# Order of work inside the slots of a selective scan: decays, first columns and the chain that makes dt

## The chip, the cores and the metric

The kernel runs on one NeuronCore of one Trainium2 chip. Its engines are named as the profile names them: PE (TensorE, matmuls; PEld is its weight load), DVE (VectorE), ACT (ScalarE), POOL (GpSimd) and SP (SyncE, which here issues nearly all DMAs). Each engine works off its own queue in order: an instruction that waits holds up everything behind it on that engine. The metric is the device time of one launch in microseconds (us), the median of several runs.

## What is computed

A network of four layers (each an attention-like block and a feed-forward block with a layer norm after each) on an input of 2 x 1024 x 1024 in float32. Only layer 2's first block, a selective state-space scan over 1024 time steps, matters here. Cut to its core:

```python
def _selective_scan(x, dt, A, Bm, Cm):
    def step(h, inp):
        x_t, dt_t, B_t, C_t = inp
        dA = jnp.exp(dt_t[..., None] * A)
        dBx = dt_t[..., None] * B_t[:, None, :] * x_t[..., None]
        h = dA * h + dBx
        y = jnp.einsum('bdn,bn->bd', h, C_t)
        return (h, y)
    h0 = jnp.zeros((x.shape[0], x.shape[1], A.shape[1]), dtype=x.dtype)
    _, ys = lax.scan(step, h0, (xT, dtT, BT, CT))
    return jnp.transpose(ys, (1, 2, 0))
...
dt = jax.nn.softplus(dt + dt_bias[None, :, None])
ys = _selective_scan(xc, dt, A, Bm, Cm)
y = (ys + D_param[None, :, None] * xc) * jax.nn.silu(z)
return jnp.einsum('bdl,hd->blh', y, out_proj_w)
```

There are 2048 channels d with 16 states n each, so 32,768 recurrences of 1024 steps for each batch element.

## The kernel before, in words

The two batch elements are done one after the other, all layers of one before the next (`net_kernel`). `l2_attn` does the scan of one batch element. Time is cut into two halves of 512 steps, u=0 and u=1; channels into 16 chunks c of 128. A chunk of one half is worked off in eight **slots**; a slot k is 128 x 2 recurrences: a tile `h` of 128 partitions (8 channels x 16 states) by 2 x 512 steps, whose two parts are called m=0 and m=1. So a batch element has 2 x 16 x 8 = 256 slots, and a run-in of 23 slots before them. All tiles of a slot, and where they come from:

- `rows(k)` (L1269) loads `h` from DRAM: dt times x of 16 channels (`dxd`), each row repeated for the 16 states (DMA at L1273, 512 KB). Nine such buffers exist.
- `times_b(k)` (L1278) multiplies it by B on POOL (L1279).
- `decay(k, m)` (L1283): a matmul (L1286) spreads dt's channels over the partitions into a PSUM bank, in two parts `hl` that carry dt's high and low bits; ACT then takes exp with scale A in place (L1288). For u=1 ACT also adds the state that u=0 left (`hst`), times the first decay, to the first column of `h` (L1291): the "first-column operation". A scan always starts from zero, so this carries the state over.
- `scan(k, m)` (L1293) is one DVE instruction (L1296): h = dA * h + h along the 512 steps.
- `keep(k)` (L1300) saves the last column for u=1 (L1304, u=0 only); `times_c(k)` multiplies by C on DVE (L1307); `states(k)` (L1311) sums over the 16 states by matmuls with a selection matrix (L1318), and a first matmul (L1316) adds D times x; `y_out` (L1328) multiplies by the gate and stores.

The chain that makes dt for a chunk is `l2_dt` (L1208), called 16 slots ahead of the chunk's first slot. Its matmul (L1211) gives the argument of the softplus; the rest is put off to later slots with `at(slot, function)`: softplus(p) is relu(p) + ln(1 + exp(-|p|)) with a correction of the rounding in 1 + exp(-|p|). `act1` and `act2` are three ACT operations each (L1221 to L1228), `pool1` two on POOL (L1231, L1232), `sum1` adds relu (L1235), `times_x` multiplies by x (L1238) and stores `dxd` in four DMAs (L1240); `parts` casts dt into the high part of `hl` (L1247), `rest` takes the low part (L1252), and `send` copies it into place by two DMAs (L1258). The tile `one` of this chain has one buffer, which `y_out` uses too.

The order of the work is written out by hand: inside `manual_schedule`, every engine's queue has the order in which the program issues. A slot issues, in this order: `rows(k+6)`, `times_b(k+2)`, `keep(k-1)`, a projection matmul (`pe()`); then scan(k,0), decay(k+1,0), the functions that were put off to this slot (`late.pop(k)`), another projection matmul; then scan(k,1), decay(k+1,1), and `states` and `times_c(k-1)`. The projection matmuls belong to other work that fills PE during the scans: the gates z (copied out by ACT at L1414), the next half's x (a convolution on DVE, L1124, and a silu), the output projection (L1441); `silu_z` (L1384) does silus between two loads of activation tables (L1388, L193). They put their later steps off with `at` as well. All PSUM tiles of the kernel, the decays' among them, come from one pool of eight banks (L43, `ps()` at L70).

Of the kernel before, what the change touches and what calls it, by code (L numbers as in the profile page):

```python
# [11 lines left out]
AF = mybir.ActivationFunctionType  # L12
# [15 lines left out]
class Net:  # L28
# [1032 lines left out]
    def l2_attn(self, b, ready, last):  # L1061
        nc, i = self.nc, self.i
        NCH, N, NR = 16, 16, 64
        NF = NR + 2 * N
        SL = 8 * NCH
        with (
# [24 lines left out]
            hst = lp.tile([P, NCH * N], F, name=self.nm("hst"))  # L1091

            def tmp(tag, bufs=2, n=HALF):
                return tp.tile([P, n], F, tag=tag, bufs=bufs, name=self.nm(tag))

            def dram(tag, shape, dtype=F):
                return [[self.dp.tile(shape, dtype, name=self.nm(tag)) for _ in range(NCH)] for _ in range(2)]

            xcd, yd = [dram(t, [P, HALF]) for t in ("xcd", "yd")]
# [3 lines left out]
            px, norms, hl, hs, dA, py, xs = {}, {}, {}, {}, {}, {}, {}  # L1103
# [6 lines left out]
            def at(k, f, *args):  # L1110
                late.setdefault(k, []).append((f, args))
# [96 lines left out]
            def l2_dt(u, c, k):  # L1208

                p = self.ps()  # L1210
                nc.tensor.matmul(  # L1211
                    p, wd[c // 8][: NF + 1, (c % 8) * P : (c % 8 + 1) * P], norms[u][0], start=True, stop=True
                )
                xs[u, c] = xc = tmp("xi")
                at(k + 3, nc.sync.dma_start, xc, xcd[u][c][:])
                e, one, lg = tmp("e", 1), tmp("one", 1), tmp("lg", 1)
                dt, dtx = lg, e
                rl = tmp("rl", 1)

                def act1():  # L1220
                    nc.scalar.activation(rl, p, AF.Relu)  # L1221
                    nc.scalar.activation(e, p, AF.Abs)
                    nc.scalar.activation(e, e, AF.Exp, scale=-1.0)

                def act2():
                    nc.scalar.activation(one, e, AF.Identity, bias=self.one)
                    nc.scalar.activation(lg, one, AF.Ln)
                    nc.scalar.activation(one, one, AF.Identity, bias=neg)  # L1228

                def pool1():  # L1230
                    nc.gpsimd.tensor_tensor(e, e, one, ALU.subtract)  # L1231
                    nc.gpsimd.tensor_tensor(lg, lg, e, ALU.add)  # L1232

                def sum1():
                    nc.gpsimd.tensor_tensor(dt, lg, rl, ALU.add)  # L1235

                def times_x():
                    nc.gpsimd.tensor_tensor(dtx, dt, xc, ALU.mult)  # L1238
                    for j in range(4):
                        nc.sync.dma_start(dxd[u][c][:, j, :], dtx[32 * j : 32 * j + 32, :])  # L1240

                low = [None]

                def parts():

                    hl[u, c] = tp.tile([P, 2, HALF], R, tag="hl", bufs=2, name=self.nm("hl"))
                    nc.scalar.copy(hl[u, c], dt.unsqueeze(1).to_broadcast([P, 2, HALF]))  # L1247

                def rest():

                    lo = low[0] = tp.tile([P, HALF], R, tag="lo", bufs=1, name=self.nm("lo"))
                    nc.gpsimd.tensor_tensor(lo, dt, hl[u, c][:, 0, :].bitcast(F), ALU.subtract)  # L1252

                def send():

                    lo = low[0]
                    for j in range(2):
                        nc.sync.dma_start(  # L1258
                            hl[u, c][64 - 64 * j : P - 64 * j, j, :].bitcast(F), lo[64 * j : 64 * j + 64, :].bitcast(F)
                        )  # L1260

                for n, f in ((1, act1), (2, act2), (3, pool1), (4, sum1), (5, times_x), (7, parts), (7, rest), (8, send)):
                    at(k + n, f)


            def of(k):
                return k // SL, k % SL // 8, k % 8 // 2, k % 2
# [15 lines left out]
            def decay(k, m):  # L1283
                u, c, q, jj = of(k)
                dA[k, m] = self.ps()
                nc.tensor.matmul(dA[k, m], rep[:, 4 * m + q, :], hl[u, c][:, jj, :], start=True, stop=True)  # L1286
                g = 16 * c + 4 * q + 2 * jj + m
                nc.scalar.activation(dA[k, m], dA[k, m], AF.Exp, scale=A[:, g : g + 1])  # L1288
                if u:
                    h0 = hs[k][:, m, 0:1]  # L1290
                    nc.scalar.activation(h0, dA[k, m][:, 0:1], AF.Identity, scale=hst[:, g : g + 1], bias=h0)  # L1291

            def scan(k, m):  # L1293
                u, c, q, jj = of(k)
# [33 lines left out]
            def y_out(k):  # L1328
                u, c = k // SL, k % SL // 8
                sz = zt.pop((u, c))  # L1330
                yo = tmp("one", 1)
                nc.scalar.copy(yo, py.pop((u, c)))
                nc.gpsimd.tensor_tensor(sz, sz, yo, ALU.mult)
                nc.sync.dma_start(yd[u][c][:], sz)
# [127 lines left out]
            with self.tc.manual_schedule():  # L1462

                todo, ahead = [], []

                def take(units, lead):
                    for n, (load, calls) in enumerate(units):
                        ahead.append((len(todo) - lead, load))
                        todo.extend(calls)

                z0, z1, x1 = gates(0), gates(1), ins(1)
                take(z0[:2] + x1[:6], 20)
                for n in range(2, 12, 2):
                    take(z0[n : n + 2] + x1[n + 4 : n + 6], 20)
                take(xproj(1), 4)
                take(z0[12:] + z1[:6], 20)
                taken = 0
                at(-BEFORE, lambda: at(4 - BEFORE, l2_spread, 0, l2_norm(0)))
                for k in range(-BEFORE, 2 * SL + 6):
                    if -16 <= k < 2 * SL - 16 and k % 8 == 0:  # L1480
                        l2_dt((k + 16) // SL, (k + 16) % SL // 8, k)
                    if k == SL + 12:
                        o = outs(0)
                        for n, (a, z) in enumerate(((6, 10), (10, 12), (12, 16), (16, 16))):
                            take(o[8 * n : 8 * n + 8], 8)
                            take(z1[a:z], 20)
                    if k == -1 or k == SL:
                        l2_cr(max(k, 0) // SL)
                    n = 3 if k < -1 else 2
                    batch = []  # L1490
                    for _ in range(n):
                        while ahead and ahead[0][0] <= taken:
                            ahead.pop(0)[1]()
                        if taken < len(todo):
                            batch.append(todo[taken])
                            taken += 1

                    def pe(last=False):
                        while batch and (last or len(batch) > n - 1):
                            f, *args = batch.pop(0)  # L1500
                            if f:
                                f(*args, k)

                    live = 0 <= k < 2 * SL
                    if 0 <= k + 6 < 2 * SL:
                        rows(k + 6)
                    if 0 <= k + 2 < 2 * SL:
                        times_b(k + 2)
                    if 0 <= k - 1 < 2 * SL:
                        keep(k - 1)  # L1510
                    pe()
                    for m in range(2):
                        if live:
                            scan(k, m)
                        if 0 <= k + 1 < 2 * SL:
                            decay(k + 1, m)
                        if m:
                            break
                        for f, args in late.pop(k, []):
                            f(*args)  # L1520
                        pe(True)
                    if k % 2 == 1 and 0 <= k - 2 < 2 * SL:
                        states(k - 2)
                    if 0 <= k - 1 < 2 * SL:
                        times_c(k - 1)
                    if live and k % 8 == 4:
                        at(k + 8, y_out, k)
                    if live and k % 8 == 0:
                        skip(k // SL, k % SL // 8)
                while late:  # L1530
                    for f, args in late.pop(min(late)):
                        f(*args)
# [460 lines left out]
```

## Time and profile before

| | us |
|---|---|
| median of 3 runs (lowest, highest) | 5127.48 (5123.48, 5133.85) |
| the profiled execution | 5130.32 |
| its span, first to last instruction | 5128.4 |
| scan stage of the first batch element | about 1050 to 2005 |
| scan stage of the second | about 3600 to 4547 |
| busy in the whole span: PE, DVE, ACT, POOL | 4706.3, 3128.0, 2109.7, 2097.7 |

The overview of the page cuts the span into 40 slices of 128 us; each digit is a slice's busy share in tenths:

```profile
PE   8989989998897888999999999899888988899999
DVE  5453256389999997225365422652899999963153
ACT  2431232377677774001024311424776777720010
POOL 2013121078798885100020220200887998831010
DMA  2144212388889998201111432113888899971100
```

In the rest of the kernel PE is busy nearly all the time; in the two scan stages all five rows are high at once. In the rows of groups, the first numbers after the bar are busy us and mean ns of one instruction; after the second bar stands the idle time of the engine just before them, with the instruction that ended most of it. In rows of the timeline the columns are start and duration in us, engine, line, operation, tiles and shapes, count, and in brackets idle time before it and its releaser. A busy PE is modelled and not a PE at its peak.

### The profile page before, as it was taken

To read this page: it belongs to the slowest core of one execution; us is meant where nothing else is said; L and a number is where in the kernel's file an instruction comes from. 1 tells how busy PE (TensorE), PEld (TensorE's weight loads), DVE (VectorE), ACT (ScalarE), POOL (GpSimd) and SP (SyncE) were. 2 spreads that over 40 slices of the span, in tenths; PEclk is the share of its full clock that TensorE was granted. 3 is DMA by queue.
4 is the path that set the end of the run, shared out by engine and by line. 5 is a ranking of instruction groups with operands and counts; after the bars stand their busy time and mean duration, and the time that the engine had idled before them with its cause. 6 is when DMAs were issued, how large, how long until landed. Compare 5 with 4: busy or idle time off the path is not lost. (4 is left out here: it accounts for less than half of the span.)

```text
span 5128.4 us, 50257 instructions
## 1 busy us (share of the span) xinstructions
PE 4706.3 (92%) x16584; PEld 2237.2 (44%) x16584; DVE 3128.0 (61%) x4322; ACT 2109.7 (41%) x4485; POOL 2097.7 (41%) x1259
## 2 busy tenths in 40 slices
PE   8989989998897888999999999899888988899999
PEld 3347645433332333455433576554333333344544
DVE  5453256389999997225365422652899999963153
ACT  2431232377677774001024311424776777720010
POOL 2013121078798885100020220200887998831010
PEclk9999999999999999999999999999999999999999
DMA  2144212388889998201111432113888899971100
GB/s 88 36 159 143 97 48 81 131 216 217 220 225 242 236 244 226 90 33 46 49 67 38 173 119 89 54 51 103 220 219 224 214 247 245 249 210 65 55 20 33
DMA packets 254871, 708.06 MB, mean 138 GB/s; under 512 B 37008, under 2 KB 54544, under 8 KB 254612
## 3 DMA queue, kind: packets, MB, share of 16 engines
q1 hardware_dynamic: 248340, 683.88, 46.7%
q0 software_dynamic: 6272, 20.98, 1.2%
q8 instruction: 133, 2.18, 0.2%
q14 instruction: 126, 1.03, 0.1%
HBM read 599.60 MB, written 86.25 MB: 134 GB/s over the span
## 5 line engine op out<-in xcount | busy, mean ns | idle before, releaser
L1296 DVE TENSOR_TENSOR_SCAN h<-ps,h 128x512 f32<-128x512 f32 x1024 | 1204.1, 1207 | 88.9 <-ACT h L1291 47.2
L1279 POOL TENSOR_TENSOR h<-h,br 128x1024 f32<-128x1024 f32 x512 | 1201.0, 2367 | 43.3 <-DMA h<-dxd 20.7
L1286 PE MATMUL ps<-hl,rep 128*128 128x512 f32 x1024 | 717.9, 708 | 119.9 <-DVE h L1296 94.7
L1288 ACT ACTIVATE ps<-ps,l_Alog 128x512 f32<-128x512 f32 x1024 | 667.9, 657 | 216.9 <-PE ps L1286 213.6
L1307 DVE TENSOR_TENSOR h<-h,ps 128x1024 f32<-128x1024 f32 x512 | 610.8, 1193 | 0.0
L1403 PE MATMUL ps<-xT,w 128*128 128x512 f32 x1024 | 541.1, 615 | 10.2 <-DVE h L1296 7.9
L1608 POOL TENSOR_TENSOR x<-x,row 128x1024 f32<-128x1024 f32 x48 | 112.3, 2349 | 796.0 <-PE ps L130 796.0
L1286 PEld LDWEIGHTS ps<-hl,rep 128*128 128x128 f32 x1024 | 198.6, 195 | 523.6 <-DVE h L1296 340.1
L152 DVE TENSOR_TENSOR x<-x,ps 128x512 f32<-128x512 f32 x192 | 128.4, 681 | 434.4 <-PE ps L1785 145.6
L1318 PE MATMUL ps<-h,sel 128*32 128x512 f32 x2048 | 365.1, 638 | 18.8 <-DVE h L1307 18.2
L104 PE MATMUL ps<-xT,w 128*128 128x512 f32 x768 | 336.1, 592 | 0.0
L177 ACT ACTIVATE rs<-mv 128x1 f32<-128x1 f32 (+2 forms) x88 | 17.9, 203 | 705.7 <-DVE mv L171 705.4
L1441 PE MATMUL ps<-w,w 128*128 128x512 f32 x512 | 279.9, 630 | 20.8 <-DMA w<-yd 12.1
L1403 PEld LDWEIGHTS ps<-xT,w 128*128 128x128 f32 x1024 | 190.6, 195 | 204.2 <-issue 136.7
L104 PE MATMUL ps<-w,xT 128*128 128x512 f32 (+1 forms) x768 | 278.3, 522 | 0.0
L1124 DVE SCALAR_TENSOR_TENSOR ps<-xp,l_convw,ps 128x512 f32<-128x512 f32 x192 | 144.4, 752 | 213.4 <-ACT ps L1119 208.9
L767 POOL TENSOR_TENSOR s<-s,l1r 128x512 f32<-128x512 f32 x64 | 66.5, 1040 | 487.7 <-DVE l1r L766 481.8
L1349 PE MATMUL ps<-xT,w 128*128 128x512 f32 x512 | 251.9, 602 | 0.7
L1291 ACT ACTIVATE h<-ps,h,hst 128x1 f32<-128x1 f32 x512 | 180.0, 352 | 118.5 <-POOL h L1279 93.9
L1782 PE MATMUL ps<-w,xT 128*128 128x512 f32 x512 | 227.4, 597 | 0.0
L1622 PE MATMUL ps<-w,w 128*128 128x512 f32 x512 | 222.6, 594 | 4.2 <-DMA w<-yd 4.2
L104 PEld LDWEIGHTS ps<-xT,w 128*128 128x128 f32 x768 | 144.8, 189 | 183.4 <-issue 177.6
(289 smaller groups left out, 7319.9 us busy)
## 6 DMA issues: line engine op xcount, KB each, us to landing
h<-dxd SPq DMA_DIRECT2D x512, 512.0 KB, 7.2
w<-l_in SPq DMA_DIRECT2D x128, 512.0 KB, 6.7
w<-l_out SPq DMA_DIRECT2D x96, 512.0 KB, 6.2
w<-l_conv SPq DMA_DIRECT2D x54, 512.0 KB, 3.9
w<-cvd SPq DMA_DIRECT2D x36, 512.0 KB, 3.3
w<-l_fw SPq DMA_DIRECT2D x32, 512.0 KB, 4.4
xcd<-xo SPq DMA_DIRECT2D x64, 256.0 KB, 2.2
xi<-xcd SPq DMA_DIRECT2D x64, 256.0 KB, 5.4
```

What stands on the lines that cost most here:

```text
L104: self.nc.tensor.matmul(out, lhsT, rhs, start=j == 0, stop=j == n - 1)
L1279: nc.gpsimd.tensor_tensor(hs[k], hs[k], norms[of(k)[0]][1].unsqueeze(1).to_broadcast([P, 2, HALF]), ALU.mult)
L1286: nc.tensor.matmul(dA[k, m], rep[:, 4 * m + q, :], hl[u, c][:, jj, :], start=True, stop=True)
L1288: nc.scalar.activation(dA[k, m], dA[k, m], AF.Exp, scale=A[:, g : g + 1])
L1296: nc.vector.tensor_tensor_scan(hs[k][:, m, :], dA.pop((k, m)), hs[k][:, m, :], 0.0, ALU.mult, ALU.add)
L1307: nc.vector.tensor_tensor(hs[k], hs[k], norms[of(k)[0]][3].unsqueeze(1).to_broadcast([P, 2, HALF]), ALU.mult)
L1318: nc.tensor.matmul(py[u, c][32 * j : 32 * j + 32, :], self.sel[:, q, :], hs[k - 1 + j // 2][:, j % 2, :], start=False, stop=q == 3,)
L1349: nc.tensor.matmul(p, w["w"][:, k * P : (k + 1) * P], self.xcols(k, u0, HALF), start=k == 0, stop=k == KD - 1)
L1403: nc.tensor.matmul(p, w["w"][:, k * P : (k + 1) * P], self.xcols(k, u * HALF, HALF), start=k == 0, stop=k == KD - 1)
L1441: nc.tensor.matmul(p, y[:, cc, t * P : (t + 1) * P], wt[:, cc * HALF : (cc + 1) * HALF], start=c2 == 0 and cc == 0, stop=last,)
L1622: nc.tensor.matmul(acc[tt], y[:, cc * HALF + tt * P : cc * HALF + (tt + 1) * P], w[:, cc * HALF : (cc + 1) * HALF], start=c == 0, stop=c = ...
L1782: nc.tensor.matmul(p, self.xcols(k, tt * P, P), wt[k][:, ns], start=k == 0, stop=False)
```

## The change

Three things in `l2_attn` and a buffer that they need. No operation is added or dropped.

- Decays: scan(k,0) is followed by decay(k+1,1) and scan(k,1) by decay(k+2,0), instead of decay(k+1,0) and decay(k+1,1).
- First columns: both of slot k+1 are issued together by a new `begin(k+1)`, after scan(k,0) and decay(k+1,1) and ahead of the functions put off to the slot.
- The chain of dt: its ACT operations take five slots (1 to 5, two operations in the first) instead of two, POOL's two log operations slots 5 and 6 instead of both in 3; the sum comes in slot 7 instead of 4, `times_x` in 8 instead of 5, `parts` in 8 instead of 7, `rest` in 9 instead of 7, `send` in 10 instead of 8. x is loaded in slot 4 instead of 3. The product with x is written to `one` instead of `e`, and `y_out` has a buffer of its own, `yo`.

```diff
@@ l2_dt(u, c, k)
-                at(k + 3, nc.sync.dma_start, xc, xcd[u][c][:])
+                at(k + 4, nc.sync.dma_start, xc, xcd[u][c][:])
                 e, one, lg = tmp("e", 1), tmp("one", 1), tmp("lg", 1)
-                dt, dtx = lg, e
+                dt, dtx = lg, one
                 rl = tmp("rl", 1)
 
                 def act1():
                     nc.scalar.activation(rl, p, AF.Relu)
                     nc.scalar.activation(e, p, AF.Abs)
+
+                def act2():
                     nc.scalar.activation(e, e, AF.Exp, scale=-1.0)
 
-                def act2():
+                def act3():
                     nc.scalar.activation(one, e, AF.Identity, bias=self.one)
+
+                def act4():
                     nc.scalar.activation(lg, one, AF.Ln)
+
+                def act5():
                     nc.scalar.activation(one, one, AF.Identity, bias=neg)
 
                 def pool1():
                     nc.gpsimd.tensor_tensor(e, e, one, ALU.subtract)
+
+                def pool2():
                     nc.gpsimd.tensor_tensor(lg, lg, e, ALU.add)
...
-                for n, f in ((1, act1), (2, act2), (3, pool1), (4, sum1), (5, times_x), (7, parts), (7, rest), (8, send)):
+                for n, f in (
+                    (1, act1), (2, act2), (3, act3), (4, act4), (5, act5), (5, pool1), (6, pool2), (7, sum1),
+                    (8, times_x), (8, parts), (9, rest), (10, send),
+                ):
                     at(k + n, f)
@@ decay(k, m)
-                if u:
+
+            def begin(k):
+                u, c, q, jj = of(k)
+                g = 16 * c + 4 * q + 2 * jj
+                for m in range(2 * u):
                     h0 = hs[k][:, m, 0:1]
-                    nc.scalar.activation(h0, dA[k, m][:, 0:1], AF.Identity, scale=hst[:, g : g + 1], bias=h0)
+                    nc.scalar.activation(
+                        h0, dA[k, m][:, 0:1], AF.Identity, scale=hst[:, g + m : g + m + 1], bias=h0
+                    )
@@ y_out(k)
-                yo = tmp("one", 1)
+                yo = tmp("yo", 1)
@@ the loop over the slots
                     for m in range(2):
                         if live:
                             scan(k, m)
-                        if 0 <= k + 1 < 2 * SL:
-                            decay(k + 1, m)
+                        if 0 <= k + 1 + m < 2 * SL:
+                            decay(k + 1 + m, 1 - m)
+                        if m == 0 and 0 <= k + 1 < 2 * SL:
+                            begin(k + 1)
                         if m:
                             break
```

## The prediction, made before the changed kernel ran

> **What bounds the kernel now.** I read the page first, then the busy time by stretch, then what the scans waited for, then the timeline ahead of single waits. Slices 8 to 16 and 25 to 35 of the page have VectorE (DVE) at nine tenths: these are the two selective-scan stages, one for each batch element. The change is in them alone.
>
> ```profile
> L1296 DVE TENSOR_TENSOR_SCAN h<-ps,h 128x512 f32<-128x512 f32 x1024 | 1204.1, 1207 | 88.9 <-ACT h L1291 47.2
> L1279 POOL TENSOR_TENSOR h<-h,br 128x1024 f32<-128x1024 f32 x512 | 1201.0, 2367 | 43.3 <-DMA h<-dxd 20.7
> L1288 ACT ACTIVATE ps<-ps,l_Alog 128x512 f32<-128x512 f32 x1024 | 667.9, 657 | 216.9 <-PE ps L1286 213.6
> ```
>
> ```profile
> 1050.00:1375.00 325.00, 283.60 (x883) 107.87 (x881) 308.26 (x286) 234.64 (x448) 274.99 (x147) 0.97 0.83 221
> 1535.00:2005.00 470.00, 396.74 (x1242) 148.32 (x1242) 443.18 (x401) 340.85 (x676) 400.98 (x213) 0.95 0.93 240
> ```
>
> The second view gives length, then PE, weight loads, DVE, ACT and POOL busy, then granted clock, DMA share and GB/s. DVE is busy 94 to 95%. Undisturbed, the timeline repeats two scans and the product with C every 3.36 us (scans start at 1519.57, 1522.93, 1526.29). POOL is next. In the whole stage DVE stands idle before scans for 88.9 us; that is all a better order can win, 1.7%. The source view of the scans says until what:
>
> ```profile
>   ACT h L1291: 47.2, 63
>   ACT ps L1288: 31.4, 28
>   DMA dxd<-e: 5.7, 1
>   POOL h L1279: 2.1, 1
> ```
>
> So ACT comes last, though it is busy only some 70%. Why is in the timeline:
>
> ```profile
> 1711.62 0.35 ACT L1291 ACTIVATE h<-ps,h,hst 128x1 f32<-128x1 f32 x1
> ...
> 1711.99 1.28 ACT L1388 ACT_TABLE_LOAD   x1
> ...
> 1713.29 1.15 ACT L1388 ACTIVATE row<-row 128x512 f32<-128x512 f32 x2
> ...
> 1714.46 1.28 ACT L193 ACT_TABLE_LOAD   x1
> ...
> 1715.75 0.66 ACT L1288 ACTIVATE ps<-ps,l_Alog 128x512 f32<-128x512 f32 x1
> 1716.45 0.35 ACT L1291 ACTIVATE h<-ps,h,hst 128x1 f32<-128x1 f32 x1
> ...
> 1716.83 1.22 DVE L1296 TENSOR_TENSOR_SCAN h<-ps,h 128x512 f32<-128x512 f32 x1 [2.34 <-ACT h L1291]
> ```
>
> A burst of other ACT work (a silu between two table loads, 3.8 us) stands in ACT's queue ahead of the decay's exp and first column for the slot's second scan, which comes 2.34 us late. I walked the timeline back from every such wait:
>
> - ACT burst with a silu: 38.7 us in 32 waits (22.7 in first halves u=0, 16.0 in u=1).
> - Burst of dt's three activations, or another copy: 12.9 us in 34 waits.
> - Waits for times_b (L1279) on POOL and the second scan after them: 17.3 us, all in u=1.
> - The first scan of each stage: 11.4. TensorE (PE) late, mostly where u changes: 7.3.
>
> They sum to 87.6. About two thirds fall before a slot's second scan (57.9 us), whose operands are queued behind the burst.
>
> **The change part by part.** No instruction is added or removed: 1024 exps, 512 first-column operations, and 64 of each operation of dt's chain stay, at the same sizes. One SBUF buffer is added (yo). Only places in queues move.
>
> *Decays half a slot sooner.* The burst of slot k now precedes exp(k+2,0), wanted at the start of slot k+2, instead of exp(k+1,1), wanted one scan (1.12 us pitch) after the start of k+1: 2.24 us more room. In u=0 no wait of a silu was over 2.33 us, so its 22.7 go, and dt's 12.9 (longest 1.5) go. In u=1, two first columns now stand behind exp(k+2,1): after the burst come two exps and one first column (0.66 + 0.66 + 0.25) instead of one and one (0.95), so some 0.6 to 0.95 of the room goes back and 1.3 us remain. The twelve silu waits of u=1 (0.6 to 2.34) leave 2.7 us. dt's cast to two parts (L1247, 1.04 us) moves from slot 7 to slot 0 of its chunk, where four of them had a silu already: plus 4. Left: 7. Gain: 38.7 + 12.9 - 7 = 44.6 us.
>
> Is the sooner exp possible at all? In the Trainium skill, "Perfetto Trace Analysis", section Optimization Strategy, a gap that repeats on the engine that should be saturated can mean that no buffer is free for the next tile. That speaks against the change: a decay needs a PSUM bank, all tiles share eight, and now three decays are alive instead of two. The trace has such waits: decay matmuls (L1286) and their weight loads sat idle until a scan 434.8 us, 560 times. By the rule the 51.6 us stay. By the rows of the timeline the bursts are solid ACT work with no wait on PE in them, while waits with PE as the last cause are 7.3 us. I take the rows. A decay now waits longer for its bank in PE's queue; behind it are projection matmuls and states(), for which the copies of z and the loads of h wait. PE needs per slot two projection matmuls with a decay each (period 1.09 us at 1508.31, 1509.41, 1510.50), 0.53 for states and 0.22 for dt and D: 2.9 of 3.36 us, so the wait is its slack. Cost between 0 and one recovered PE wait a chunk; I take 0.
>
> *First columns together, half a slot ahead.* begin(k+1) waits for times_b(k+1), as the first column of m=0 did before, at the same scan. Behind it wait the late operations and exp(k+2,0) instead of exp(k+1,1). When POOL is late, the second scan no longer pays for it: the 4.1 us of second waits go.
>
> *dt's chain one operation a slot.* POOL had four 1.27 us operations in slots 3 and 4 (two of dt's log, y's product, the sum); now one a slot in 5, 6, 7, 0, 1 and y's in 4. xi is loaded at slot 4 and used at 8, instead of 3 and 5: POOL's 24.3 us (11 times) of waiting for xi end. POOL needs per eight slots 8 x 2.34 + 6 x 1.27 = 26.3 us, against DVE's 26.9: it can hold the pace, but hardly catches up. Of POOL's 13.2 us I count a third, 4.4, off, half-way between none (POOL stays as late) and two thirds (the xi waits explain most): with the second waits, 8.5 gained.
>
> Against it: times_x moves from slot 5 to 8, its four writes dxd (1.73 us of SP) behind the row load of k+14, and the next chunk's first row is read at slot 10, so SP holds everything queued there (weights, rows) until dxd has landed. In u=1 times_x ends 6.2 us after its slot's first scan, issues take 1.9, dxd lands in 2.9 (median), a row in 9.5:
>
> ```profile
> h<-dxd SPq DMA_DIRECT2D x52, 512.0 KB, 9.5
> ```
>
> Sum 20.5 us after slot 8. times_b must end by some 0.7 us ahead of slot 16: 8 x 3.4 - 0.7 - 2.4 = 24.1. Slack 3.6 us. The longest row took 14.3, 4.8 more, so a tail pays. "DMA: Bandwidth & Descriptors", section Anatomy of one DMA, gives 2.0 us plus bytes over 436 GB/s, fitted on the software path: 2.2 for dxd and 3.2 for a row, estimated sum 13.5 and no cost. The row's 9.5 is measured here under this stage's load, so I use it. Bounds: 0, and 62 chunks x 1.2 us = 74 (a quarter of the tail's 4.8 in every chunk); I take 6, a tenth of the chunks at 1 us each, since POOL has lead there. The two sends of hl move on SP from slot 8 to slot 10, behind that first row (1.15 us to issue, landing in at most 11.7); their decay is wanted by slot 15: hidden behind five slots, 17 us, and if SP were 4 us late PE would stand at that decay. At the stage's start slots are paced by PE (8 in 21.5 us) and two of them, 5.4 us, cover issue and landing of dxd (1.7 + 2.9): 0, at worst +5 a stage.
>
> **Sum.** 44.6 + 8.5 - 6 = 47 us. The profiled execution took 5130.3 (span 5128.4 and 1.9 around it), 2.8 over the median of 5127.5. 5127.5 - 47 = 5080.
>
> **Rivals.**
> A, POOL and DMA become the bound. For: u=1 has POOL waits of some 50 us beyond its 401 busy, DMA share is 0.93 there, and faster slots raise demand from 240 towards 250 GB/s. Then u=1 keeps its length, its 43 us of ACT and POOL waits turned into waits for POOL and DMA, and only the 25 us of bursts in u=0 are gained: 5103. Against: half of POOL's waits are those of an engine ahead.
> B, the change doesn't do what it says: banks, not queue order, time the exps. Only the POOL part remains: 8.5 - 6, about 5125. Against: the solid bursts.
> C, slower: the two-slot gap between times_x and the first row read. If the chain is typically 4.8 us longer than its medians, 62 chunks stall 1.2 us each: 74 - 53 = 21 lost, 5148. It decides from 0.86 us a chunk (53 / 62). For: SP in order, rows of 9.5 us. Against: 3.6 us of slack.
>
> **How the numbers follow.** Forecast (5055 to 5095) 0.57, A 0.19, B 0.12, C 0.12. 0.2% of the time, 10 us, is about what measuring this kernel can tell from no change: faster is below 5117, slower above 5138. A forecast and most of A are faster, 0.75; B and edges same, 0.13; C slower, 0.12. The range reaches from 5052 (75 us gained, all but the first scans) to 5128, where B ends; beyond it lie C and a little.
>
> **What would show it.** Right: idle before L1296 falls from 88.9 to about 40 us; waits behind silu and dt bursts vanish in u=0 and shrink in u=1; L1238's wait for xi goes; PE's waits at L1286 grow without harm. Wrong: DVE waits on times_b at the first slot of each chunk, with L1279 idle until h<-dxd well above 20.7 us (C); POOL near 97% busy in u=1 with DVE still idle (A); idle before L1296 unchanged with ACT idle before L1288 (B).

## The result, and the profile after

| | median, us | ratio to before, 95% interval |
|---|---|---|
| before, 5 runs | 5127.48 | |
| after, 5 runs | 5167.24 | 1.0074 [1.0056, 1.0091] |

The changed kernel is slower, by 40 us where 47 us less were forecast. Its profiled execution took 5171.16 us with a span of 5169.4, so the two profiled executions differ by 40.8 us. In the line numbers of the changed kernel the scan is L1313, times_b L1290, the decay's matmul L1297, its exp L1299, the first columns L1306, keep L1321, times_c L1324 and the first matmul of y L1333.

The rows of groups on the page of the changed kernel that answer to those of before; ahead of them stands the row of times_c of the kernel before:

```profile
L1307 DVE TENSOR_TENSOR h<-h,ps 128x1024 f32<-128x1024 f32 x512 | 610.8, 1193 | 0.0
```

```profile
L1313 DVE TENSOR_TENSOR_SCAN h<-ps,h 128x512 f32<-128x512 f32 x1024 | 1196.0, 1205 | 58.5 <-ACT h L1306 41.4
L1290 POOL TENSOR_TENSOR h<-h,br 128x1024 f32<-128x1024 f32 x512 | 1206.2, 2368 | 44.5 <-DMA h<-dxd 21.2
...
L1299 ACT ACTIVATE ps<-ps,l_Alog 128x512 f32<-128x512 f32 x1024 | 675.8, 668 | 467.4 <-PE ps L1297 465.7
L1324 DVE TENSOR_TENSOR h<-h,ps 128x1024 f32<-128x1024 f32 x512 | 611.2, 1194 | 70.9 <-ACT hst L1321 70.9
```

Nothing got longer in itself: scans 1205 ns against 1207, times_b 2368 against 2367. Idle time before scans fell from 88.9 to 58.5 us. But the product with C, which never waited in the kernel before (its row ends in 0.0), now waits 70.9 us for ACT, for the tile `hst`, which is the copy of the last column. The account closes: -30.4 + 70.9 = +40.5 us. The row of L1299 says where ACT lost its time: the exps' idle time, nearly all of it a wait for PE, rose from 216.9 to 467.4 us.

The busy time of the two stretches that the prediction used, of the changed kernel:

```profile
1050.00:1375.00 325.00, 271.27 (x833) 101.66 (x831) 283.55 (x263) 214.10 (x415) 256.17 (x138) 0.94 0.73 197
1535.00:2005.00 470.00, 400.72 (x1259) 149.04 (x1258) 446.45 (x405) 329.06 (x693) 418.74 (x225) 0.92 0.92 242
```

In the first stretch, all u=0, DVE's busy time fell from 308.26 to 283.55, and everything else with it; the second, nearly all u=1, is a little fuller than before (446.45 against 443.18). So first halves lost and second halves gained. From the start times of the scans: u=0 took 484.3 and 482.3 us for the two batch elements before, 507.7 and 509.0 after; u=1, to the last product with C, 470.4 and 464.7 before, 465.0 and 459.6 after. That is +50 and -10.5 (which part of the change the -10.5 belong to is taken up below).

What the scans of the changed kernel waited for, from the source view:

```profile
  ACT h L1306: 41.4, 28
  ACT ps L1299: 16.7, 10
```

In u=0 DVE's idle time before scans fell from 40.6 to 16.7 us, of which 11.4 are the first scans of the two stages: the bursts no longer delay a scan there. The 22 new waits of times_c are regular. In both batch elements, every 16 slots, one of about 4.84 us comes at slot 12, 28, 44, 60, 76, one of about 2.05 at 16, 32, 48, 64, 80, and there is one of 0.66 at slot 1. The timeline of the changed kernel ahead of the first long one:

```profile
1096.75 1.55 DVE L1124 SCALAR_TENSOR_TENSOR ps<-xp,l_convw,ps 128x512 f32<-128x512 f32 x2
1098.20 1.22 DVE L1313 TENSOR_TENSOR_SCAN h<-ps,h 128x512 f32<-128x512 f32 x1
...
1099.48 1.72 PE L1333 MATMUL ps<-xi,dg 128*128 128x512 f32 x2 [2.85 <-DVE h L1313]
...
1101.13 1.93 PE L1335 MATMUL ps<-h,sel 128*32 128x512 f32 x8
...
1102.99 1.25 PE L1366 MATMUL ps<-xT,w 128*128 128x512 f32 x2
...
1103.68 0.80 PE L1297 MATMUL ps<-hl,rep 128*128 128x512 f32 x1
...
1104.52 0.66 ACT L1299 ACTIVATE ps<-ps,l_Alog 128x512 f32<-128x512 f32 x1 [4.82 <-PE ps L1297]
...
1106.23 1.28 ACT L1129 ACT_TABLE_LOAD   x1
...
1109.18 1.28 ACT L193 ACT_TABLE_LOAD   x1
...
1110.47 0.66 ACT L1299 ACTIVATE ps<-ps,l_Alog 128x512 f32<-128x512 f32 x1
1111.06 0.18 ACT L1321 COPY hst<-h 128x2 f32<-128x2 f32 x1
...
1111.28 1.22 DVE L1324 TENSOR_TENSOR h<-h,ps 128x1024 f32<-128x1024 f32 x1 [4.84 <-ACT hst L1321]
```

And the same place of the kernel before:

```profile
1095.04 2.31 DVE L1124 SCALAR_TENSOR_TENSOR ps<-xp,l_convw,ps 128x512 f32<-128x512 f32 x3
...
1095.17 1.13 PE L1316 MATMUL ps<-xi,dg 128*128 128x512 f32 x2 [1.74 <-DVE h L1296]
...
1106.40 1.22 DVE L1296 TENSOR_TENSOR_SCAN h<-ps,h 128x512 f32<-128x512 f32 x1 [2.32 <-ACT ps L1288]
...
1107.54 1.20 DVE L1307 TENSOR_TENSOR h<-h,ps 128x1024 f32<-128x1024 f32 x1
```

Read them side by side. In slot 11 the y of the second chunk (its slot 3) asks for a PSUM bank, for its first matmul. Before, that matmul started as scan(11,0) ended, beside the convolution's three taps on DVE (L1124, 2.31 us). After, it waits for scan(11,1), which stands behind the taps (the view shows the last two of them): one scan and the taps later. Behind it in PE's queue are the state sums (L1335), a projection (L1366) and the next decay (L1297), so that ACT sits idle 4.82 us. Then the burst with the silu (two table loads) comes, then the exp that is now half a slot sooner, and only then keep. keep reads the last column of `h`, and times_c overwrites `h` in place, so DVE has to wait for it. u=1 keeps no last column, and there DVE never waits before times_c.

The banks in which the scheduler put the tiles, in the built programs, agree: y's first matmul in u=0 takes a bank that scan(k,1) of the same slot leaves in 10 of 32 chunks after (slots 11, 27, 43, 59, 75 of each batch element), in none before. In u=0 most decays (346 of 512 before, 314 after) take the bank of the fourth decay ahead of them; a decay asked for half a slot sooner holds its bank longer, and others get one that is released later.

**The theory** to be tested: the sooner decays take bank time away; PE, in order, waits for later scans; the exps and the burst behind them are late; keep is behind one exp more, and so the wait lands on times_c. **Rivals**: only keep's place in ACT's queue does it, without banks; the new chain of dt does it; the row reads or the start do it. A lower clock can be set aside from the traces: PE's granted clock in u=0 was 0.97 before and 0.95 and 0.94 after, but in the 21 us ahead of the first long stall (1075 to 1096) it was 1.00 in both kernels, and in u=1, with 0.95 before and 0.92 and 0.94 after, the changed kernel was the faster one.

### The profile page after: what moved, and what is told of

The parts are those of the page before. It is cut to its first block, busy times and chain, and to the rows that moved or that the text cites. A ratio compares the mean times of both kernels' runs of the same rounds, so it can differ in the third digit from the quotient of the medians.

```text
span 5169.4 us, 50099 instructions
## 1 busy us (share of the span) xinstructions
PE 4694.7 (91%) x16584; PEld 2225.6 (43%) x16584; DVE 3125.1 (60%) x4322; ACT 2054.2 (40%) x4485; POOL 2093.4 (40%) x1259
## 5 line engine op out<-in xcount | busy, mean ns | idle before, releaser
L1313 DVE TENSOR_TENSOR_SCAN h<-ps,h 128x512 f32<-128x512 f32 x1024 | 1196.0, 1205 | 58.5 <-ACT h L1306 41.4
L1290 POOL TENSOR_TENSOR h<-h,br 128x1024 f32<-128x1024 f32 x512 | 1206.2, 2368 | 44.5 <-DMA h<-dxd 21.2
L1297 PE MATMUL ps<-hl,rep 128*128 128x512 f32 x1024 | 699.7, 689 | 182.9 <-DVE h L1313 143.6
L1299 ACT ACTIVATE ps<-ps,l_Alog 128x512 f32<-128x512 f32 x1024 | 675.8, 668 | 467.4 <-PE ps L1297 465.7
L1324 DVE TENSOR_TENSOR h<-h,ps 128x1024 f32<-128x1024 f32 x512 | 611.2, 1194 | 70.9 <-ACT hst L1321 70.9
L1420 PE MATMUL ps<-xT,w 128*128 128x512 f32 x1024 | 554.6, 629 | 15.9 <-DVE h L1313 8.1
L1297 PEld LDWEIGHTS ps<-hl,rep 128*128 128x128 f32 x1024 | 200.5, 198 | 638.1 <-DVE h L1313 450.5
L104 PE MATMUL ps<-xT,w 128*128 128x512 f32 x768 | 336.2, 592 | 0.0
L1335 PE MATMUL ps<-h,sel 128*32 128x512 f32 x2048 | 313.1, 656 | 4.0 <-DVE h L1324 3.5
L1124 DVE SCALAR_TENSOR_TENSOR ps<-xp,l_convw,ps 128x512 f32<-128x512 f32 x192 | 144.5, 753 | 212.1 <-ACT ps L1119 207.5
L1366 PE MATMUL ps<-xT,w 128*128 128x512 f32 x512 | 253.7, 605 | 0.0
L99 ACT COPY xT<-ps 128x512 f32<-128x512 f32 x128 | 75.4, 590 | 344.2 <-PE ps L130 344.2
```

The costliest lines, as they stand in the source:

```text
L104: self.nc.tensor.matmul(out, lhsT, rhs, start=j == 0, stop=j == n - 1)
L1290: nc.gpsimd.tensor_tensor(hs[k], hs[k], norms[of(k)[0]][1].unsqueeze(1).to_broadcast([P, 2, HALF]), ALU.mult)
L1313: nc.vector.tensor_tensor_scan(hs[k][:, m, :], dA.pop((k, m)), hs[k][:, m, :], 0.0, ALU.mult, ALU.add)
L1324: nc.vector.tensor_tensor(hs[k], hs[k], norms[of(k)[0]][3].unsqueeze(1).to_broadcast([P, 2, HALF]), ALU.mult)
L1335: nc.tensor.matmul(py[u, c][32 * j : 32 * j + 32, :], self.sel[:, q, :], hs[k - 1 + j // 2][:, j % 2, :], start=False, stop=q == 3,)
L1366: nc.tensor.matmul(p, w["w"][:, k * P : (k + 1) * P], self.xcols(k, u0, HALF), start=k == 0, stop=k == KD - 1)
```

## The experiments

Each was timed beside the kernel before, in five rounds. A ratio is to before; us of a ratio are taken at 5127.5.

| run | median, us | ratio, 95% interval | idle before scans, before times_c, us |
|---|---|---|---|
| order_only | 5192.02 | 1.0124 [1.0109, 1.0139] | 59.7, 64.2 |
| chain_only | 5117.45 | 0.9976 [0.9967, 0.9985] | 80.3, 0.0 |
| second_half | 5112.73 | 0.9969 [0.9956, 0.9981] | 81.5, 0.0 |
| keep_early | 5146.02 | 1.0033 [1.0020, 1.0046] | 52.6, 53.5 |
| before_7banks | 5245.02 | 1.0223 [1.0210, 1.0237] | 200.7, 0.0 |
| before_9banks | 5428.11 | 1.0577 [1.0563, 1.0591] | 171.3, 0.0 |
| after_9banks | 5465.66 | 1.0648 [1.0629, 1.0666] | 15.0, 7.7 |
| taps_later | 5138.28 | 1.0010 [0.9999, 1.0020] | 51.7, 54.6 |
| y_sooner | 5109.62 | 0.9959 [0.9945, 0.9972] | 42.1, 29.7 |
| y_sooner_before | 5174.01 | 1.0082 [1.0069, 1.0096] | 123.1, 0.0 |
| y_taps_keep | 5088.06 | 0.9925 [0.9912, 0.9939] | 40.1, 12.8 |
| chain_y | 5092.60 | 0.9928 [0.9915, 0.9942] | 60.3, 0.0 |
| chain_y_taps | 5077.85 | 0.9907 [0.9888, 0.9926] | 43.7, 0.0 |
| cast_later | 5086.84 | 0.9923 [0.9905, 0.9941] | 39.2, 8.3 |
| after_7banks | 5297.23 | 1.0336 [1.0315, 1.0357] | 158.1, 94.7 |

### Which part loses: order_only, chain_only

Before with the new order of decays and first columns; and after with the old one:

```diff
-                        if 0 <= k + 1 < 2 * SL:
-                            decay(k + 1, m)
+                        if 0 <= k + 1 + m < 2 * SL:
+                            decay(k + 1 + m, 1 - m)
+                        if m == 0 and 0 <= k + 1 < 2 * SL:
+                            begin(k + 1)
```

> Before with the decays half a slot sooner and the first columns together, the chain of dt left as it was. Banks (the third live decay takes a PSUM bank away, PE's queue waits for later scans, the exps and with them the copy of the last column come late): the loss is in this part, so the products with C stand idle about 70 us in the first halves, and the time is 5155 to 5170. Chain of dt (the moved dt operations cost, and the decays alone would have gained what I forecast): 5080 to 5100, no idle time before the products with C. Start or DMA: as before, 5127.

> The new chain of dt, the load of x a slot later and the buffer yo, with decays and first columns in the old order. Banks: this part costs nothing and gains at most the 8.5 us of POOL's waits, 5115 to 5130. Chain of dt: the whole loss is here, about 5165. Gap between times_x and the first row: 5140 or more, with the first product with B of a chunk waiting for its row.

Measured: 1.0124 and 0.9976. The page's row of times_c in order_only:

```profile
L1313 DVE TENSOR_TENSOR h<-h,ps 128x1024 f32<-128x1024 f32 x512 | 613.5, 1198 | 64.2 <-ACT hst L1310 63.8
```

The loss is in the order of the decays alone, and a little larger there than in the whole change (64 us against 38 by the ratios; the forecast said up to 5170, so it was too low). It lies in u=0 again (508.7 and 505.6 us there, 467.1 and 464.8 in u=1), where no first column is touched, so putting the first columns together is not what costs. The wait for keep comes with it: 4.32 us in each of the ten long places, and 1.09 at slots 16, 32 and so on, where dt's cast has not been moved. The new chain of dt is a gain of 12 us (8 to 17), so the second rival falls, and so does the third: chain_only has the same two-slot gap and the same start.

### Which half: second_half

After, with the old order in u=0:

```diff
-                        if 0 <= k + 1 + m < 2 * SL:
-                            decay(k + 1 + m, 1 - m)
+                        new = k + 1 >= SL
+                        if not new:
+                            if 0 <= k + 1:
+                                decay(k + 1, m)
+                        elif k + 1 + m < 2 * SL:
+                            decay(k + 1 + m, 1 - m)
+                        if k + 2 == SL and m:
+                            decay(k + 2, 0)
```

> After, but with the old order of decays in the first halves u=0; new order in u=1 only, new chain everywhere. Banks and last column: no last column is kept in u=1, so the products with C stand idle nowhere; the first halves are as long as before (about 483 us from first scan to first scan), the second halves as short as after (465, 460): 5110 to 5120. Chain of dt: the first halves stay as long as after (507), 5160.

Measured: 0.9969, no idle time before times_c, halves of 482.5, 463.1, 480.6 and 461.6 us, as forecast. Against chain_only (0.9976) the sooner decays in u=1 are worth 4 us with an interval of some 8 either way: no difference that these runs can tell. In the profile of chain_only u=1 took 456.0 and 464.7 us, in sum 4 less than after (465.0 and 459.6): the new chain alone accounts for what the second halves gained.

### Is it only keep's place: keep_early

```diff
-                    if 0 <= k - 1 < 2 * SL:
-                        keep(k - 1)
...
                         if live:
                             scan(k, m)
+                        if live and m:
+                            keep(k)
```

> After, with the copy of the last column issued on ACT right behind its scan, ahead of the next decay's exp instead of behind it. Place of the copy in ACT's queue alone: one exp of 0.66 us with its wait for PE no longer stands between, the 70.9 us before the products with C go for the most part, 5100 to 5115. Banks: at the long stalls the exp ahead of the copy comes directly after a burst that is itself late because PE was late, so only the 0.66 us of the exp is gained in each of the 22 stalls, some 10 to 15 us: 5150 to 5160.

Measured: 1.0033, 21 us better than after, just below the banks' range and far from the other's. The page's row of times_c:

```profile
L1324 DVE TENSOR_TENSOR h<-h,ps 128x1024 f32<-128x1024 f32 x512 | 613.3, 1198 | 53.5 <-ACT hst L1321 53.5
```

Three quarters of times_c's wait stay. The long stalls shrink from 4.84 to 4.27 us (two of the ten to 2.96) and the others from 2.05 to 1.19, about one exp each, as worked out; ACT's idle time for PE ahead of the burst is still 4.25 us at slot 12. keep's place is the smaller share; the late burst is the larger.

### What a bank costs: before_7banks, after_7banks

One bank is held through the stages by a tile that nothing else uses.

```diff
                 taken = 0
+                held = self.ps()
+                nc.scalar.copy(held[:, 0:1], neg)
...
+                nc.scalar.copy(neg, held[:, 0:1])
```

> Before with one of the eight PSUM banks held idle through both scan stages; order as before. Banks: a bank less is what the third live decay takes from the other tiles, so the first halves get longer by 10 us or more each and PE waits longer for scans at the decays: 5145 to 5175. Place of the last column's copy alone: one bank less does not matter, 5125 to 5135.

> After, with one of the eight PSUM banks held idle through both scan stages. Banks: the bank costs more than the 115 us that it costs in the old order, since three decays are alive: 5300 or more. If the loss of after is not one of banks but of ACT's order: the bank costs about the same, 115, so 5270 to 5290, or less.

Measured: 1.0223 and 1.0336. The page's row of the scan in before_7banks, and then the rows of the scan and of times_c in after_7banks:

```profile
L1296 DVE TENSOR_TENSOR_SCAN h<-ps,h 128x512 f32<-128x512 f32 x1024 | 1210.8, 1211 | 200.7 <-ACT ps L1288 89.6
```

```profile
L1313 DVE TENSOR_TENSOR_SCAN h<-ps,h 128x512 f32<-128x512 f32 x1024 | 1198.5, 1210 | 158.1 <-ACT h L1306 115.6
...
L1324 DVE TENSOR_TENSOR h<-h,ps 128x1024 f32<-128x1024 f32 x512 | 613.9, 1199 | 94.7 <-ACT hst L1321 94.7
```

A bank less costs 114 us in the old order, three times the loss of the change and far above the 5145 to 5175 of the forecast: banks are what this stage is short of. In the old order the shortage shows at exps and scans alone; times_c never waits. In the new order it costs 1.0336 - 1.0074 = 0.0262, 134 us. The difference of 20 us has an interval of about 16 either way: a bank is somewhat dearer in the new order, but not by as much as I had expected.

### A bank more, by way of SBUF: before_9banks, after_9banks

C is left in SBUF, so that its PSUM bank is free.

```diff
-                norms[u][3] = self.ps()
-                nc.scalar.copy(norms[u][3], norms[u][2])
+                norms[u][3] = norms[u][2]
...
-                br, cr = tmp("br"), tmp("cr", 1)
+                br, cr = tmp("br"), tmp("cr", 2)
```

(A small scratch tile of the norm shares another's buffer, to make room.)

> Control. Before, with C kept in SBUF instead of a PSUM bank, so the other tiles have one bank more; the product with C on DVE then reads both operands from SBUF, as POOL's product with B does. If that costs DVE or POOL nothing: 5115 to 5130, products with C at 1.19 us as before. If the two engines hinder each other in SBUF: the two products get longer than 1.19 and 2.37 us, and the time is above 5130.

> After, with C kept in SBUF, which gives the freed bank to the third live decay. Banks: the idle time before the products with C falls from 70.9 us to under 20, and the kernel is 20 to 50 us faster than the control with C in SBUF and the old order. Place of the copy alone: the 70.9 us stay within 15, and it is some 40 us slower than that control.

Measured: 1.0577 and 1.0648. The control became 296 us slower, so the pair says little on banks. The page's row of times_c in before_9banks, and then in after_9banks:

```profile
L1306 DVE TENSOR_TENSOR h<-h,cr 128x1024 f32<-128x1024 f32 x512 | 819.9, 1601 | 0.0
```

```profile
L1323 DVE TENSOR_TENSOR h<-h,cr 128x1024 f32<-128x1024 f32 x512 | 1013.4, 1979 | 7.7 <-ACT hst L1320 7.7
```

In the new order DVE then hardly waits at all (15.0 and 7.7 us, where the control waits 171.3), which is what the bank theory says; but its products have grown by 194 us more than the control's, and that kernel is the slower one. The forecast that it would beat its control is wrong. The slower pace gives PE more time too, so the vanished waits are no proof.

### The taps: taps_later

```diff
-                            at(now + 2, lambda: l2_taps(c, p, w["x"]))
+                            first[now + 3] = lambda: l2_taps(c, p, w["x"])
```

(`first` is worked off at the start of a slot, ahead of scan(k,0).)

> After, with the three taps of the next half's convolution (2.3 us on DVE) put after scan(k,1), ahead of the next slot's first scan, instead of between the two scans of a slot. Banks: at the long stalls the first matmul of y waits for scan(k,1), which then ends 2.3 us sooner; the ten stalls of 4.84 us lose about 2.3 each, the others stay: 5135 to 5150. Place of the copy alone: the taps only change places with a scan, so the stalls stay at 4.84 and 2.05: 5160 to 5170.

Measured: 1.0010, 33 us better than after by the ratios. The page's row of times_c:

```profile
L1324 DVE TENSOR_TENSOR h<-h,ps 128x1024 f32<-128x1024 f32 x512 | 613.8, 1199 | 54.6 <-ACT hst L1321 54.6
```

The long stalls fall from 4.84 to 2.9 us, by 1.9 where 2.3 were expected; those at 16, 32 and so on stay at 2.05 to 2.35. So scan(k,1)'s end is what PE waits for there: ending it sooner ends the stall sooner.

### The wait itself: y_sooner and its control

y's bank is held from slot 3 of its chunk to slot 12, counted from the chunk's first slot; the next chunk's y asks at slot 11. Copying it out in slot 10, after its last matmuls in slot 9, frees one in time:

```diff
-                        at(k + 8, y_out, k)
+                        at(k + 6, y_out, k)
```

> After, with y copied out of its PSUM bank in slot 10 of its chunk instead of slot 12, right after its last matmuls. The bank comes free before the next chunk's y asks for one at slot 11, so that in u=0 no first matmul of y gets the bank of a scan(k,1) (ten did). Banks: the ten stalls of 4.84 us at slots 12, 28 and so on fall to 1 us or less, the eleven of about 2 us at 16, 32 and so on stay: 5115 to 5135. Place of the copy alone: the burst ahead of it is only shorter by y's copy, 0.59 us in ten places: 5155 to 5165.

> Control: the same for the kernel before. Banks: there y's first matmul got the bank of a scan(k,0) that had ended, and the exps have more room; some of the 8 us of waits in which PE was last may go: 5115 to 5130. If y's place in ACT's bursts is what matters, its silu bursts get shorter by 0.59 in each chunk, and the 22.7 us of u=0 fall by up to 6: 5115 to 5125. The control is to show that the gain of the other run belongs to the new order.

Measured for y_sooner: 0.9959, below the kernel before, and 59 us better than after. The timeline of y_sooner at the place shown above:

```profile
1096.37 1.13 PE L1333 MATMUL ps<-xi,dg 128*128 128x512 f32 x2 [0.66 <-DVE h L1313]
...
1100.26 0.66 ACT L1299 ACTIVATE ps<-ps,l_Alog 128x512 f32<-128x512 f32 x1 [0.31 <-PE ps L1297]
...
1106.31 0.18 ACT L1321 COPY hst<-h 128x2 f32<-128x2 f32 x1
...
1106.53 1.22 DVE L1324 TENSOR_TENSOR h<-h,ps 128x1024 f32<-128x1024 f32 x1
```

y's first matmul again starts beside the taps, the exp ahead of the burst waits 0.31 us instead of 4.82, and times_c waits 0.14 us instead of 4.84, in all ten places. The burst itself is only shorter by y's copy, 0.59 us. In the built program no y of u=0 takes the bank of a scan(k,1) any more. With taps_later, which ends that scan sooner and leaves the banks alone, this settles the cause of the ten long stalls: y's wait for a bank that scan(k,1) still holds. The stalls at 16, 32 and so on stay, at 2.05 to 3.52 us. In u=0 of the first batch element PE and its weight loads waited at y's first matmul for scans 36.0 us before, 43.9 after and 10.8 here: between before and after the sum says little, since before the wait was for a scan that ended a scan and the taps sooner.

The control got slower, 1.0082, which neither forecast had. Its source view of the chain's operation that writes `one` (L1226) shows why:

```profile
  POOL row L1333: 41.5, 30
  POOL zo L1333: 40.7, 28
```

In the old chain, `one` has a single buffer that y's copy uses too; in slot 10 that copy falls on the chain's own slot, and ACT waits 82.2 us for POOL to finish with it (before: 0). This control was ill made. The clean one is chain_y, which has the buffer `yo`.

### With the repairs, is the order worth anything: y_taps_keep, chain_y, chain_y_taps, cast_later

y_taps_keep is after with the last three edits (y, taps, keep). chain_y and chain_y_taps are chain_only with the edit of y, and with those of y and taps.

> After with the three repairs: y copied out in slot 10, the taps after scan(k,1), the last column's copy ahead of the next exp. Banks: with y's wait gone, the taps no longer ahead of a scan and 0.6 to 0.9 us off each other stall, the products with C stand idle under 15 us and the first halves take 475 us or less: 5080 to 5105, below the kernel before. If the loss were PE's lack of time and not banks: the stalls move to other waits, 5120 or more.

> The old order of decays with the new chain of dt and y copied out in slot 10. Compared with the run of all three repairs it shows whether the sooner decays are worth anything once their stalls are repaired. If so, this one stays at 5105 to 5120 and the other is below 5100; if the order is worth nothing, both are alike within 10 us.

> Old order of decays, new chain of dt, y copied out in slot 10, the taps after scan(k,1); the only difference to the kernel with all three repairs is the order of decays and first columns and the copy of the last column, which stalls nothing in the old order. If the sooner decays are worth something once repaired: this one is 5095 to 5110, slower than that one's 5088. If they are worth nothing: within 8 us of it, or faster. The silu bursts still stand before scans in the old order (about 20 us over both first halves).

Measured: 0.9925, 0.9928 and 0.9907. The three repairs do what was forecast, but for one first half of 479.3 us where 475 was the bound (the other took 472.1), and take 76 us off the changed kernel. But the old order gets as far with y's edit alone. The page's row of times_c in y_taps_keep, where the scans wait 40.1 us besides, and then the row of the scan in chain_y_taps, where times_c never waits:

```profile
L1324 DVE TENSOR_TENSOR h<-h,ps 128x1024 f32<-128x1024 f32 x512 | 612.5, 1196 | 12.8 <-ACT hst L1321 12.8
```

```profile
L1307 DVE TENSOR_TENSOR_SCAN h<-ps,h 128x512 f32<-128x512 f32 x1024 | 1200.6, 1214 | 43.7 <-ACT h L1302 26.8
```

DVE's waits add up to 52.9 us in the one and 43.7 in the other: in both orders the scans come undisturbed for the most part. With the chain of dt new in all of them, the price of the sooner decays is the difference of two ratios: 0.0098 (50 us) with y in slot 12, 0.0031 (16 us) with y in slot 10, 0.0018 (9 us) with the taps moved too (and keep put early, in the new order alone), each with about 0.002 (10 us) either way. So most of the order's loss went with y's bank, and with all three repairs the order is worth nothing measurable, since in the old order too the burst waits of u=0 are gone by then: 16.8 us of idle time before scans are left in the first halves of chain_y_taps (40.6 before), 13.1 of them at the first scans. chain_y_taps has the lowest ratio of all runs, 0.9907 of before, though its interval touches that of y_taps_keep.

The stalls of 2.05 us at slots 16, 32 and so on hold dt's cast to two parts (L1255, 1.04 us) in front of the silu's burst. cast_later puts it a slot later:

```diff
-                    (8, times_x), (8, parts), (9, rest), (10, send),
+                    (8, times_x), (9, parts), (10, rest), (11, send),
```

> The kernel with all three repairs, and the cast of dt to two parts a slot later, in slot 9 of the chain instead of slot 8, where it stands in front of the silu's burst (rest and send follow, in 10 and 11). If the cast makes the remaining stalls at slots 16, 32 and so on: ten stalls of 1.19 us lose 1.04 each, idle before the products with C falls from 12.8 to about 3 us, 5075 to 5085. If PE makes them: they stay at about 1.2, 5085 to 5092.

Measured: 0.9923. The stalls, 1.19 us after keep's edit, become 0.22 to 0.64, so the cast makes most of them, as the 1.09 us in order_only had hinted. But those at slot 1 grew from 0.47 to 1.12 and one of 2.75 us came up at slot 95: the row fell from 12.8 only to 8.3, and the time can't be told from y_taps_keep's.

## Why the prediction was wrong, point by point

**Bank waits.** This is the step that failed: "so the wait is its slack. Cost between 0 and one recovered PE wait a chunk; I take 0." In its place the runs show a price: the sooner decays, which were to gain 44.6 us, cost 50 us with y in slot 12 (after against chain_only, 10 either way). I averaged PE's need over a slot (2.9 of 3.36 us) and set that against a queue in which a single late bank delays everything behind it. The pages' rows of the decays' matmuls and weight loads, before and then after:

```profile
L1286 PE MATMUL ps<-hl,rep 128*128 128x512 f32 x1024 | 717.9, 708 | 119.9 <-DVE h L1296 94.7
L1286 PEld LDWEIGHTS ps<-hl,rep 128*128 128x128 f32 x1024 | 198.6, 195 | 523.6 <-DVE h L1296 340.1
```

```profile
L1297 PE MATMUL ps<-hl,rep 128*128 128x512 f32 x1024 | 699.7, 689 | 182.9 <-DVE h L1313 143.6
L1297 PEld LDWEIGHTS ps<-hl,rep 128*128 128x128 f32 x1024 | 200.5, 198 | 638.1 <-DVE h L1313 450.5
```

Their idle time for scans grew from 94.7 + 340.1 = 434.8 to 143.6 + 450.5 = 594.1 us, as I had said that it would, but not "without harm": exps waited for PE 250 us more. At times_c 70.9 us reached DVE (keep's place and dt's cast have a share in them), and in u=1 about 16 us at scans whose exp had come late from PE. I also looked for free banks only for the decays, not for y, which asks for one in slot 11. The rule that I had set aside (the Trainium skill, "Perfetto Trace Analysis", Optimization Strategy: a repeating gap can mean that no buffer is free) was the better guide to the change than the rows of single waits, which showed what was late before and not what would be late next.

**keep.** The prediction listed what stands behind an exp that is put sooner for scans and first columns, and left out keep, which sits there too, and times_c, which must wait for it. No rival named it. The 70.9 us are the whole sign of the result.

**Bursts in u=0.** Right: idle time before scans fell from 40.6 to 16.7 us there, and without the first scans of the stages from 29.2 to 5.3. Over both halves it fell to 58.5 us, where about 40 were forecast; the rest is u=1.

**u=1.** Wrong in what it gave to the order of the decays. The waits, sorted by what stood ahead of them on ACT: silu bursts 16.0 to 11.7 us (2.7 to 6.7 expected), dt's bursts gone, POOL 17.3 to 6.8 (8.8 expected), but some 16 us of waits for PE, and 7 us behind an operation of dt's chain (next point). The sum is 47.7 before and 41.7 after. The 10.5 us that u=1 gained are not the order's: order_only gained 3 us there, chain_only 14.

**The chain of dt.** It gained, but not by the sum. Of the 8.5 us that were expected of POOL, 4.1 stood under the first columns; the chain's own entries were 4.4 gained and 6 paid. Measured are 12 us gained (8 to 17) in chain_only, and POOL's wait for xi is gone (24.3 us before). The 6 us of chain lateness weren't paid: times_b waited for rows 21.2 us against 20.7, with rows of 7.8 us (median over u=1) where the sum took 9.5 from a stretch of 200 us (over the whole of u=1 it was 8.5). A cost that stood nowhere in the prediction came with the new buffer: the product with x is written to `one`, so the next chunk's third operation (L1228), which writes `one` too, waits until that product has been stored. In the second half of the first batch element the waits view of ACT has (us in total, times, longest):

```profile
ACT one L1228 <- DMA dxd<-one: 8.7, 3, 5.9
```

In the whole run that is 24.2 us in 9 waits (none at the same operation before, L1226), of which the scans of u=1 got 7.4; in chain_only, 23.2 us in 8. No run gave the product a buffer of its own.

**Rivals.** A is wrong: in u=1 of the first batch element POOL was busy 403 of 465 us (87%), where nearly 97 would have been its sign. C is wrong, as the rows' 21.2 us show. B had the right resource and the wrong price: it let banks cancel the gain, and gave no way in which they make a loss.

**Left open.** Whether the order would gain with a ninth bank; there are eight, and freeing C's makes DVE and POOL collide. The 16 us for PE and the 7 behind L1228 in u=1 were read from the trace and not tested apart, and neither was a buffer for the product with x. With y alone repaired the sooner decays still cost 16 us (10 either way); how that divides between the cast, keep and u=1 was not settled. How much of the old order's gain from chain_y to chain_y_taps (0.0021, 11 us, with 12 either way) is the taps', and by what way, was not traced.

## What to carry to other kernels

Before moving work sooner, count who holds a bank (or any buffer of a shared pool) in each slot, for all tiles of the pool, and look for the slot where the count is highest; there the added hold time can turn into waits of others, through an in-order queue and at nearly full length (4.82 of ACT and 4.84 us of DVE here), whatever the average slack. List everything that is queued behind a moved instruction, the small copies too, and who must wait for them, above all who overwrites a tile in place. And try shortening a long hold first: copying y out two slots sooner brought 25 us in the old order, without any new order.

## What the runs showed of the hardware that was not expected

Two engines that both read SBUF hindered each other severely. With C in PSUM, DVE's product took 1193 to 1204 ns on average in every other run, and POOL's product with B 2367 to 2374. With C in SBUF the source view of after_9banks has:

```profile
L1323 DVE TENSOR_TENSOR h<-h,cr x512: 1191/2351/10264, 1061.7 to 4883.9; 128x1024 f32<-128x1024 f32 x171
```

The columns are minimum, median and maximum in ns: from undisturbed to 10.26 us, and POOL's product rose to 2656 on average (2988 in before_9banks; its longest took 3432 in both). The Trainium skill, "SBUF — State Buffer", section Who interferes with whom, says that a DVE instruction with two SBUF inputs contends with a GpSimd instruction that reads SBUF, because its second input comes over the read interface that they share; these runs agree, and price it at 296 us in 5127. The copy of C into a PSUM bank in this kernel pays for itself, even though a bank taken from the eight cost 114 us.
